# A quantile graph layer: the sorting network's VectorE operations cut to at most 384 elements, the one-element writes between them removed

## The chip, the cores and the metric

The kernel runs on one core of a Trainium2 chip. Its time is the device time of one execution in microseconds (us), the median of several runs; less is better. Besides, one execution is recorded by the hardware profiler; the profile and the trace are that one execution. The engines are called PE (TensorE, matrix products), ACT (ScalarE), DVE (VectorE), POOL (GpSimd) and SP (SyncE, which here only starts DMAs).

## The reference

There are 16 graphs of 1024 nodes with 64 features, a dense adjacency matrix for each (a random edge has a probability of 1/256 in each direction, then the matrix is made symmetric and gets its diagonal), a node mask, and a two-layer perceptron. What is computed, cut to what matters:

```python
h = jnp.maximum(_layernorm(x, axis=-1), 0.0)
# in the graph layer, x is h:
skip = jnp.where(nb > T, (nb + K - 1) // K, 1)          # T, K = 10, 2; nb = number of neighbours
rem = neigh & (sk > 1) & (rank % sk == sk - 1) & mask[:, :, None]
adj_d = jnp.where(rem | jnp.swapaxes(rem, 1, 2), 0.0, adj_)
nd = adj_d > 0
s = jnp.sort(jnp.where(nd[..., None], x[:, None, :, :], jnp.inf), axis=2)
for tau, w in zip((0.25, 0.5, 0.75), (0.25, 0.5, 0.25)):
    pos = tau * jnp.maximum(nd.sum(2) - 1, 0)
    agg = agg + w * (v_lo + frac * (v_hi - v_lo))        # the quantile, interpolated between two sorted values
y = jax.nn.relu((x + agg) @ W1 + b1) @ W2 + b2
out = x_in + y * mask
```

So for each node and each feature, the features of its remaining neighbours are sorted, and three quantiles are mixed.

## The kernel before, in words

**Preparation of a graph** (`load`, `number`, `drop`, `keep`, `order`, `collect`, `normalize`). The adjacency matrix comes in by rows on SP's queue; PE, ACT and DVE drop edges as the reference says and turn what is left into lists of neighbours. The nodes are reordered by degree into 8 blocks of 128, so that a block's nodes need about the same number of list places (`CAPS`: 13 down to 6). DVE finds the lists (L1047, L1087 to L1116); they end as columns of the index tile `idx`. The normalized features go to a table `gtab` in DRAM.

**Gathers.** For each pair of graphs, `fetch` puts one indirect DMA per graph, block and list place on POOL's queue (L1250): 128 rows of 64 floats, named by one column of `idx`, land in one slot of a tile `g`. There are 1008 of them in all. The blocks form four classes, `CLASSES = (((0,), 13), ((1, 2, 3), 11), ((4, 5), 9), ((6, 7), 7))`; a class has one tile `g`, in which a slot holds 128 elements per partition for each of the class's blocks (2 graphs x 64 features): 128, 384, 256 and 256. A few nodes of high degree are handled apart, eight graphs at a time, in a tile `gg` with slots of 128.

**The sort** (`sort`, L1271) runs over a class's tile on DVE. A plan (`PLANS`) is a list of steps; each step names up to three slots to be compared with up to three others, so that one DVE operation handles n slots. A step is a minimum and a maximum (L1288 into a free slot, L1289 in place) or, where only one result is wanted, a single operation (L1285). Then `taken` slots are multiplied by coefficients (L1296), n slots in an operation, and PE adds them into `acc` in PSUM (L1298). Sizes run from 128 to 768 elements per partition, in 32-bit floats.

**The pauses.** After the operations of a step, `let_go` (L1265) looks whether the estimated cost since the last pause has come to 0.8 us; if so it writes a zero into a one-element tile `pause` (L1268), which nobody reads.

**The order of the work.** `weave` mixes the sort of a pair of graphs (`results`, `aggregate`) with the preparation of the next pair, and hands POOL its gathers along the way (`SPREAD` paces them). Afterwards `arrange` (L640) takes all instructions, estimates each one's cost (`Step.cost`), plays the engines' queues through, and fixes the order in which every engine has its instructions. A pause is not a step of its own there: it is kept as the tail of the operation that it follows, adds its cost to it, and is put right behind it in DVE's order.

**The end.** Behind the last pair come the perceptron (`mlp`, `output`), the stores, two indirect stores for each group (L1498), and a flag that says whether any list was too short.

Of the kernel before, what the change touches and what calls it, by code (L numbers as in the profile page):

```python
# [31 lines left out]
F32 = mybir.dt.float32  # L32
# [8 lines left out]
OP = mybir.AluOpType  # L41
AX = mybir.AxisListType

P = 128
N = 1024
C = 64
# [40 lines left out]
BIG = 3.0e38  # L87

SPREAD = 160


FIRST = CAPS[0] - 1
# [508 lines left out]
class Step:  # L601

    def __init__(self, ins, place):
        self.ins, self.place, self.kind = ins, place, type(ins).__name__
        self.engine = NAMES[str(ins.engine).split(".")[-1]]
        self.reads, self.writes = (
            [Use(a.bass_ap) for a in aps if getattr(a, "bass_ap", None) is not None] for aps in (ins.ins, ins.outs)
        )
        self.moves = self.kind == "InstDMACopy"
        self.before, self.behind, self.after, self.tail = set(), set(), [], []  # L610
        self.busy, self.lag = self.cost()

    def cost(self):
# [23 lines left out]
        return 480, 1500 + by / 300  # L637


def arrange(tc, runs, tails=()):  # L640

    steps, found, number = [], {}, {}
    for ins in list(tc.nc.cur_bb.bb.instructions):
        if type(ins).__name__.startswith("BassTile"):
            continue
        if ins.name in tails:
            at = found[tails[ins.name]]
            at.tail.append(ins)
            number[ins.name] = len(number)
            at.busy += Step(ins, 0).busy  # L650
            found[ins.name] = at
            continue
        found[ins.name] = Step(ins, len(steps))
        steps.append(found[ins.name])

    written, read, users, order = {}, {}, {}, {}
    for s in steps:
        for u in s.reads + s.writes:
            name = u.tile.name
            for o, other in written.get(name, ()):  # L660
                if u.meets(other):
                    s.before.add(o.place)
            if u in s.writes:
                for o, other in read.get(name, ()):
                    if u.meets(other):
                        s.before.add(o.place)
        for u in s.writes:
            for table in (written, read):
                table[u.tile.name] = [e for e in table.get(u.tile.name, ()) if not u.covers(e[1])]
            written[u.tile.name].append((s, u))  # L670
        for u in s.reads:
            read.setdefault(u.tile.name, []).append((s, u))
        for u in s.reads + s.writes:
            if getattr(u.tile, "tag", None):
                if u.tile.name not in users:
                    order.setdefault(u.tile.tag, []).append(u.tile)
                users.setdefault(u.tile.name, []).append(s)
    for tiles in order.values():
        for k, t in enumerate(tiles):
            bufs = t.tag_meta.bufs  # L680
            first = users[t.name][0]
            if k:
                first.behind.add(users[tiles[k - 1].name][0].place)
            if k >= bufs:
                first.before.update(o.place for o in users[tiles[k - bufs].name])
            for o in users[t.name][1:]:
                if o is not first:
                    o.behind.add(first.place)
    close = {found[n].place: (found[run[0]].place, found[run[-1]].place) for run in runs for n in run[:-1]}
    for s in steps:  # L690
        for first, last in {close[p] for p in s.before if p in close}:
            if not first <= s.place <= last:
                s.before.add(last)
    for s in steps:
        s.behind -= s.before
        s.before.discard(s.place)
        s.behind.discard(s.place)
        s.left, s.ready = len(s.before) + len(s.behind), 0.0
        for p in (*s.before, *s.behind):
            steps[p].after.append(s)  # L700

    free, wire = dict.fromkeys(ENGINES, 0.0), 0.0
    waiting, able, sequence = ({e: [] for e in ENGINES} for _ in range(3))
    for s in steps:
        if not s.left:
            heappush(waiting[s.engine], (0.0, s.place))
    done = 0
    while done < len(steps):
        when, e = min(
            (free[e] if able[e] else max(free[e], waiting[e][0][0]), e) for e in ENGINES if able[e] or waiting[e]  # L710
        )
        while waiting[e] and waiting[e][0][0] <= when:
            heappush(able[e], heappop(waiting[e])[1])
        s = steps[heappop(able[e])]
        if waiting[e] and waiting[e][0][0] < when + PATIENCE and waiting[e][0][1] < s.place - AHEAD:
            heappush(able[e], s.place)
            free[e] = waiting[e][0][0]
            continue
        done += 1
        sequence[e].append(s)  # L720
        free[e] = when + s.busy
        if e == "SP":
            wire = max(wire, free[e]) + s.lag - 1500
            s.lag = wire + 1500 - free[e]
        for o in s.after:
            if s.place in o.behind:
                least = when
            else:
                least = free[e] + (s.lag + 60 if o.engine != e or s.moves else 115 if e == "DVE" else 0)
            o.ready = max(o.ready, least)  # L730
            o.left -= 1
            if not o.left:
                heappush(waiting[o.engine], (o.ready, o.place))
        for q in ENGINES:
            while waiting[q] and waiting[q][0][0] <= free[q]:
                heappush(able[q], heappop(waiting[q])[1])

    for steps in sequence.values():
        alike = iter(sorted((i for s in steps for i in s.tail), key=lambda i: number[i.name]))
        line = [i for s in steps for i in (s.ins, *(next(alike) for _ in s.tail))]  # L740
        for ins, then in zip(line, line[1:]):
            tc.add_manual_dep(
                then, ins.name, mybir.DependencyInfo(mybir.DependencyClass.NoSync, mybir.DependencyReason.DATA),
                reason="order of the engine",
            )
# [3 lines left out]
def list_layer(  # L749
# [14 lines left out]
    nc = tc.nc  # L764
# [8 lines left out]
    runs = []  # L773
# [444 lines left out]


    pairs = B // 2  # L1220
    tails = {}
    gathered, groups = {}, {}


# [35 lines left out]
                        queue.append(partial(gather, h, slot, k, PASSED[k] + s))  # L1260


    pause = cst.tile([P, 1], F32, name="pause")

    def let_go(held, ins):  # L1265
        if held < 0.8:
            return held
        tails[nc.vector.memset(pause, 0.0).ins.name] = ins.ins.name  # L1268
        return 0.0

    def sort(lines, plan, first, coef, acc):  # L1271

        size = lines.shape[2]
        held = 0.0

        def at(first, step, n):
            stop = first + step * (n - 1) + (1 if step >= 0 else -1)
            return lines[:, first:stop if stop >= 0 else None:step or 1]

        _, _, steps, ends, taken = plan  # L1280
        for n, a, da, b, db, f, df, back, what in steps:
            pa, pb = at(a, da, n), at(b, db, n)
            cost = 0.16 + n * size / 960
            if f < 0:
                ins = nc.vector.tensor_tensor(pa if back else pb, pa, pb, OP.min if what == "min" else OP.max)  # L1285
            else:
                one, other = (OP.min, OP.max) if what == "<" else (OP.max, OP.min)
                nc.vector.tensor_tensor(at(f, df, n), pa, pb, one)  # L1288
                ins = nc.vector.tensor_tensor(pa if back else pb, pa, pb, other)  # L1289
                cost *= 2  # L1290
            yield cost
            held = let_go(held + cost, ins)
        for n in taken:
            now, ends = ends[:n], ends[n:]
            v = at(now[0], now[1] - now[0] if n > 1 else 0, n).rearrange("p s (k c) -> p s k c", c=C)
            ins = nc.vector.tensor_tensor(v, v, coef(first, n)[:, :, :, None].to_broadcast(list(v.shape)), OP.mult)  # L1296
            settle([
                nc.tensor.matmul(  # L1298
                    acc, ident32, lines[:, s], start=False, stop=(s == now[-1] and not ends), skip_group_check=True
                )  # L1300
                for s in now
            ])
            first += n
            cost = 0.16 + n * size / 960
            held = let_go(held + cost, ins)
            yield cost

    def terms(acc, out):
# [283 lines left out]
    fp = psum.tile([1, 1], F32, name="fp", tag="misc")  # L1592
    nc.tensor.matmul(fp, worst, ones_col(cst, nc), start=True, stop=True)
    nc.vector.tensor_scalar(flag, fp, 0.0, None, OP.is_gt)
    arrange(tc, runs, tails)


def ones_col(pool, nc):
# [173 lines left out]
```

## Time and profile before

| what | value |
|---|---|
| time, median of 3 runs | 2607.62 us (2595.87 to 2612.22) |
| the profiled execution's own time | 1581.97 us |
| span of the profiled execution | 1580.2 us |
| granted TensorE clock, mean | 0.841 of full speed |
| DVE busy, instructions | 1191.0 us, 3723 |
| POOL busy, instructions | 1137.8 us, 1051 |
| PE, ACT busy | 1071.0 us, 917.2 us |
| gathers (L1250) | 1008, 1081 ns on the average, from 68.3 to 1516.6 us |
| pauses (L1268) | 578, 59 ns each |

The timed runs and the profiled execution differ by more than a thousand microseconds. The profile describes the second alone. Busy time is the time in which an engine has an instruction under way; an engine with 75% may still be late in one stretch and idle in another. In the groups of instructions, the number behind the bar is the busy time in all and the mean of one in nanoseconds, then the idle time of the engine just before, with what ended it; "issue" means that nothing the profile shows was waited for.

### The profile page before, as it was taken

To read this page: it belongs to the slowest core of one execution; us is meant where nothing else is said; L and a number is where in the kernel's file an instruction comes from. 1 tells how busy PE (TensorE), PEld (TensorE's weight loads), DVE (VectorE), ACT (ScalarE), POOL (GpSimd) and SP (SyncE) were. 2 spreads that over 40 slices of the span, in tenths; PEclk is the share of its full clock that TensorE was granted. 3 is DMA by queue.
4 is the path that set the end of the run, shared out by engine and by line. 5 is a ranking of instruction groups with operands and counts; after the bars stand their busy time and mean duration, and the time that the engine had idled before them with its cause. 6 is when DMAs were issued, how large, how long until landed. Compare 5 with 4: busy or idle time off the path is not lost.

```text
span 1580.2 us, 25600 instructions
## 1 busy us (share of the span) xinstructions
PE 1071.0 (68%) x8385; PEld 664.2 (42%) x8385; DVE 1191.0 (75%) x3723; ACT 917.2 (58%) x2496; POOL 1137.8 (72%) x1051
## 2 busy tenths in 40 slices
PE   6777867889887887888569845588758822602235
PEld 3444544555554555455245534354535412301122
DVE  5615489865997789868884899977988897697660
ACT  6998886987958695978367841766825300200001
POOL 3277776777777777777777777777777777777730
PEclk9989979899998999899679976899888955855568
DMA  6453432442523252325122422222311211211100
GB/s 208 118 159 93 116 110 62 113 116 64 149 69 112 53 149 58 111 59 143 50 71 73 118 78 45 73 84 56 86 28 26 46 31 26 55 24 23 22 11 18
DMA packets 128481, 122.71 MB, mean 78 GB/s; under 512 B 94514, under 2 KB 95026, under 8 KB 128338
## 3 DMA queue, kind: packets, MB, share of 16 engines
q1 hardware_dynamic: 94994, 86.77, 19.4%
q0 software_dynamic: 33344, 34.21, 9.7%
q8 instruction: 68, 1.11, 0.3%
q14 instruction: 75, 0.61, 0.1%
HBM read 110.10 MB, written 9.07 MB: 75 GB/s over the span
## 4 chain that ended last, share of the span: by engine, by line
POOL 32%; ACT 20%; PE 14%; issue 14%; DVE 12%; DMA 6%; DVEq 0%; POOLq 0%; SPq 0%; ACTq 0%
POOL g L1250 31%; PE codeP L1072 5%; DMA g<-gtab,idx 4%; ACT dist L978 4%; ACT sg L891 3%; DVE g L1288 3%; ACT ne L911 3%; DVE g L1289 2%; ACT kept L1001 2%; ACT waste L1170 2%; ACT waste L1165 1%; ACT xt L1178 1%; PE acc L1298 1%; PE rk L968 1%; DMA xt<-in_x_dram 1%
## 5 line engine op out<-in xcount | busy, mean ns | idle before, releaser
L1250 POOL DMA_INDIRECT g<-gtab,idx x1008 | 1089.7, 1081 | 361.3 <-issue 288.0
L1288 DVE TENSOR_TENSOR g<-g 128x512 f32<-128x512 f32 (+3 forms) x408 | 280.7, 701 | 40.9 <-DMA g<-gtab,idx 25.9
L1289 DVE TENSOR_TENSOR g<-g 128x512 f32<-128x512 f32 (+3 forms) x408 | 281.4, 702 | 11.1 <-DMA gg<-g 8.4
L1298 PE MATMUL acc<-g,kf 128*128 128x256 f32 (+2 forms) x448 | 143.4, 461 | 176.5 <-DVE pause L1268 105.2
L1072 PE MATMUL codeP<-pack,perm 128*128 128x332 bf16 x1024 | 185.3, 323 | 21.4 <-DVE perm L1047 18.4
L978 ACT ACTIVATE dist<-rk,bias 128x512 f16<-128x512 f32 x256 | 168.4, 698 | 27.8 <-DVE bias L953 10.7
L1298 PEld LDWEIGHTS acc<-g,kf 128*128 128x128 f32 x448 | 89.5, 231 | 204.1 <-DVE pause L1268 111.4
L968 PE MATMUL rk<-kb,cnt 128*128 128x512 bf16 x256 | 113.2, 442 | 74.5 <-ACT dist L978 68.2
L1001 ACT ACTIVATE kept<-kp 128x512 fp8e4<-128x512 f32 x248 | 149.2, 617 | 14.0 <-PE kp L996 11.9
L898 PE MATMUL tp<-kb,sg 128*128 128x128 bf16 x1024 | 106.8, 243 | 69.3 <-ACT sg L891 52.6
L911 ACT ACTIVATE ne<-tp 128x512 fp8e4<-128x512 f32 x248 | 138.2, 608 | 19.4 <-PE tp L904 10.7
L973 PEld LDWEIGHTS <-ne 128*128 128x128 fp8e4 x1024 | 90.2, 109 | 133.1 <-issue 110.8
L1072 PEld LDWEIGHTS <-perm 128*128 128x128 bf16 x1024 | 93.9, 101 | 85.3 <-DVE perm L1047 43.9
L891 ACT ACTIVATE sg<-at 128x1024 bf16<-128x1024 f32 x121 | 126.6, 1076 | 2.4 <-DMA at<-in_adj_dram 2.3
L898 PEld LDWEIGHTS <-sg 128*128 128x128 bf16 x1024 | 81.2, 110 | 91.1 <-ACT sg L891 61.1
L973 PE MATMUL rk<-kw,ne 128*128 128x128 fp8e5 x1024 | 118.0, 243 | 0.0
L979 DVE TENSOR_SCALAR rem<-dist,half 128x1024 bf16<-128x1024 f16 x128 | 64.7, 506 | 61.7 <-ACT dist L978 60.7
L996 PE MATMUL kp<-kw,rem 128*128 128x128 fp8e5 x1024 | 99.7, 219 | 0.0
L991 PE MATMUL kp<-ne,kw 128*128 128x512 fp8e4 x256 | 98.5, 385 | 0.1
L992 PE MATMUL kp<-rem,kw 128*128 128x512 bf16 x256 | 97.6, 382 | 0.0
L1077 ACT CAST st<-codeP 128x4 bf16<-128x4 f32 x128 | 21.1, 165 | 119.6 <-PE codeP L1072 119.5
L1373 DVE TENSOR_SCALAR at_p<-iota,node 128x512 bf16<-128x512 f16 x256 | 82.8, 370 | 6.8 <-PE low L1397 6.7
(178 smaller groups left out, 2051.1 us busy)
## 6 DMA issues: line engine op xcount, KB each, us to landing
at<-in_adj_dram SPq DMA_DIRECT2D x122, 512.0 KB
g<-gtab,idx POOLq DMA_INDIRECT x1008
xt<-in_x_dram SPq DMA_DIRECT2D x16, 256.0 KB
y<-in_x_dram SPq DMA_DIRECT2D x16, 256.0 KB
gtab<-xt SPq DMA_DIRECT2D x16, 256.0 KB
out_dram<-y SPq DMA_DIRECT2D x16, 256.0 KB
spare<-in_adj_dram SPq DMA_DIRECT2D x6, 512.0 KB
gg<-g SPq DMA_DIRECT2D x32, 48.0 KB
```

The lines of the kernel that those rows point to most:

```text
L891: nc.scalar.activation(sg, at, AF.Sign)
L898: run.append(nc.tensor.matmul(tp[:, s], sg[:, m * P:(m + 1) * P], ident16, start=(s == 0), stop=(s == 3 and t // 4 != n), skip_group_check ...
L911: nc.scalar.activation(to, tp, AF.Relu, saturate=False)
L968: run = [nc.tensor.matmul(rk, cnt[:, ts], blocks[:, 4 * n:4 * n + 4, None].to_broadcast([P, 4, P]), start=True, stop=False, skip_group_che ...
L973: run.append(nc.tensor.matmul(rk[:, s * P:(s + 1) * P], ne[:, 4 * n + s, ts], upper, start=False, stop=(s == 3), skip_group_check=True,))
L978: nc.scalar.activation(dist[:, n * HALF:(n + 1) * HALF], rk, AF.Abs, bias=bias[:, t:t + 1])
L1001: nc.scalar.activation(kept[:, 4 * n:4 * n + 4], kp, AF.Relu, saturate=False)
L1072: run.append(nc.tensor.matmul(flat, perm[:, t, k * P:(k + 1) * P], pack[:, t], start=False, stop=(t == NT - 1), skip_group_check=True,))
L1250: return nc.gpsimd.indirect_dma_start(out=gathered[m, tiles][:, slot, k - lo, h], out_offset=None, in_=tables[2 * m + h][0], in_offset=bas ...
L1288: nc.vector.tensor_tensor(at(f, df, n), pa, pb, one)
L1289: ins = nc.vector.tensor_tensor(pa if back else pb, pa, pb, other)
L1298: nc.tensor.matmul(acc, ident32, lines[:, s], start=False, stop=(s == now[-1] and not ends), skip_group_check=True)
```

## The change

In `sort`, every step is cut into parts of at most `PART // size` slots (at least one), where `size` is the number of elements in a slot. A part does what the step did, for its own slots. With 384 as the limit, a part holds three slots of 128, one of 256 or one of 384. The products are cut in the same way; the matrix products that add them stay together in one run behind all parts. The pauses go, with `let_go`, the tile `pause` and the tails in `arrange`.

```diff
+PART = 384
...
-def arrange(tc, runs, tails=()):
+def arrange(tc, runs):
...
-        if ins.name in tails:
-            at = found[tails[ins.name]]
-            at.tail.append(ins)
-            number[ins.name] = len(number)
-            at.busy += Step(ins, 0).busy
-            found[ins.name] = at
-            continue
...
-        alike = iter(sorted((i for s in steps for i in s.tail), key=lambda i: number[i.name]))
-        line = [i for s in steps for i in (s.ins, *(next(alike) for _ in s.tail))]
+        line = [s.ins for s in steps]
...
-    def let_go(held, ins):
-        if held < 0.8:
-            return held
-        tails[nc.vector.memset(pause, 0.0).ins.name] = ins.ins.name
-        return 0.0
...
+        most = max(1, PART // size)
+
+        def parts(n):
+            return [(k, min(most, n - k)) for k in range(0, n, most)]
+
         for n, a, da, b, db, f, df, back, what in steps:
-            pa, pb = at(a, da, n), at(b, db, n)
-            cost = 0.16 + n * size / 960
-            if f < 0:
-                ins = nc.vector.tensor_tensor(pa if back else pb, pa, pb, OP.min if what == "min" else OP.max)
-            else:
-                one, other = (OP.min, OP.max) if what == "<" else (OP.max, OP.min)
-                nc.vector.tensor_tensor(at(f, df, n), pa, pb, one)
-                ins = nc.vector.tensor_tensor(pa if back else pb, pa, pb, other)
-                cost *= 2
+            for k, many in parts(n):
+                pa, pb = at(a + k * da, da, many), at(b + k * db, db, many)
+                if f < 0:
+                    nc.vector.tensor_tensor(pa if back else pb, pa, pb, OP.min if what == "min" else OP.max)
+                else:
+                    one, other = (OP.min, OP.max) if what == "<" else (OP.max, OP.min)
+                    nc.vector.tensor_tensor(at(f + k * df, df, many), pa, pb, one)
+                    nc.vector.tensor_tensor(pa if back else pb, pa, pb, other)
+            cost = (0.16 + n * size / 960) * (1 if f < 0 else 2)
             yield cost
-            held = let_go(held + cost, ins)
...
-            ins = nc.vector.tensor_tensor(v, v, coef(first, n)[:, :, :, None].to_broadcast(list(v.shape)), OP.mult)
+            for k, many in parts(n):
+                some = now[k:k + many]
+                v = at(some[0], some[1] - some[0] if many > 1 else 0, many).rearrange("p s (k c) -> p s k c", c=C)
+                nc.vector.tensor_tensor(
+                    v, v, coef(first + k, many)[:, :, :, None].to_broadcast(list(v.shape)), OP.mult
+                )
```

More of the change, by code (lines that the diff above doesn't have):

```diff
@@ L609, in __init__ @@
         self.moves = self.kind == "InstDMACopy"
-        self.before, self.behind, self.after, self.tail = set(), set(), [], []
+        self.before, self.behind, self.after = set(), set(), []
         self.busy, self.lag = self.cost()
@@ L637, in cost @@
         return 480, 1500 + by / 300
-def arrange(tc, runs, tails=()):
-    steps, found, number = [], {}, {}
+def arrange(tc, runs):
+    steps, found = [], {}
     for ins in list(tc.nc.cur_bb.bb.instructions):
         if type(ins).__name__.startswith("BassTile"):
-            continue
-        if ins.name in tails:
-            at = found[tails[ins.name]]
-            at.tail.append(ins)
-            number[ins.name] = len(number)
-            at.busy += Step(ins, 0).busy
-            found[ins.name] = at
             continue
@@ L1220, in list_layer @@
     pairs = B // 2
-    tails = {}
     gathered, groups = {}, {}
@@ L1260, in fetch @@
                         queue.append(partial(gather, h, slot, k, PASSED[k] + s))
-    pause = cst.tile([P, 1], F32, name="pause")
-    def let_go(held, ins):
-        if held < 0.8:
-            return held
-        tails[nc.vector.memset(pause, 0.0).ins.name] = ins.ins.name
-        return 0.0
     def sort(lines, plan, first, coef, acc):
         size = lines.shape[2]
-        held = 0.0
         def at(first, step, n):
@@ L1280, in sort @@
         _, _, steps, ends, taken = plan
+        most = max(1, PART // size)
+        def parts(n):
+            return [(k, min(most, n - k)) for k in range(0, n, most)]
         for n, a, da, b, db, f, df, back, what in steps:
-            pa, pb = at(a, da, n), at(b, db, n)
-            cost = 0.16 + n * size / 960
-            if f < 0:
-                ins = nc.vector.tensor_tensor(pa if back else pb, pa, pb, OP.min if what == "min" else OP.max)
-            else:
-                one, other = (OP.min, OP.max) if what == "<" else (OP.max, OP.min)
-                nc.vector.tensor_tensor(at(f, df, n), pa, pb, one)
-                ins = nc.vector.tensor_tensor(pa if back else pb, pa, pb, other)
-                cost *= 2
+            for k, many in parts(n):
[7 more added lines that the diff above has]
+            cost = (0.16 + n * size / 960) * (1 if f < 0 else 2)
             yield cost
-            held = let_go(held + cost, ins)
         for n in taken:
             now, ends = ends[:n], ends[n:]
-            v = at(now[0], now[1] - now[0] if n > 1 else 0, n).rearrange("p s (k c) -> p s k c", c=C)
-            ins = nc.vector.tensor_tensor(v, v, coef(first, n)[:, :, :, None].to_broadcast(list(v.shape)), OP.mult)
+            for k, many in parts(n):
[4 more added lines that the diff above has]
+                )
             settle([
@@ L1304, in sort @@
             cost = 0.16 + n * size / 960
-            held = let_go(held + cost, ins)
             yield cost
@@ L1594, in list_layer @@
     nc.vector.tensor_scalar(flag, fp, 0.0, None, OP.is_gt)
-    arrange(tc, runs, tails)
+    arrange(tc, runs)
 def ones_col(pool, nc):
```

## The prediction

> **What bounds the kernel now.** I read the page first: busy shares, then the chain that ended last.
>
> ```profile
> span 1580.2 us, 25600 instructions
> ...
> PE 1071.0 (68%) x8385; PEld 664.2 (42%) x8385; DVE 1191.0 (75%) x3723; ACT 917.2 (58%) x2496; POOL 1137.8 (72%) x1051
> ...
> POOL 32%; ACT 20%; PE 14%; issue 14%; DVE 12%; DMA 6%; DVEq 0%; POOLq 0%; SPq 0%; ACTq 0%
> ```
>
> POOL leads the chain with 32%, and the 14% of "issue" is mostly POOL's too, as the line's view of the gathers shows (durations in ns: least, median, most; then what the engine sat idle for):
>
> ```profile
> L1250 POOL DMA_INDIRECT g<-gtab,idx x1008: 940/952/2609, 68.3 to 1516.6; - x168
> ...
>   issue: 288.0, 945
>   DVE idx L1116: 55.0, 3
> ```
>
> An undelayed gather costs 0.952 us and the 0.305 us gap behind it (288.0/945), 1.257 in all. From the first gather at 68.3 us to the last at 1516.6 POOL does little but that. So, in the profiled execution, POOL sets the end: 68 us to start, 1449 of gathers, 63 behind the last one. The groups by shape (busy us, mean ns | idle before) give what lengthens them:
>
> ```profile
> L1250 POOL DMA_INDIRECT g<-gtab,idx x1008 | 1089.7, 1081 | 361.3 <-issue 288.0 <-DVE idx L1116 55.0 <-DMA g<-gtab,idx 7.9
> ...
> L1289 DVE TENSOR_TENSOR g<-g 128x768 f32<-128x768 f32 x128 | 121.5, 949 | 0.6
> ...
> L1288 DVE TENSOR_TENSOR g<-g 128x512 f32<-128x512 f32 x136 | 92.6, 685 | 15.1 <-DMA g<-gtab,idx 11.5 <-issue 3.2
> ...
> L1296 DVE TENSOR_TENSOR g<-g,coef 128x768 f32<-128x768 f32 x64 | 59.2, 950 | 0.1
> ...
> L1289 DVE TENSOR_TENSOR g<-g 128x384 f32<-128x384 f32 x88 | 47.9, 550 | 8.6 <-DMA gg<-g 8.4
> ...
> L1268 DVE MEMSET pause<- 128x1 f32 x578 | 34.1, 59 | 0.0
> ```
>
> The gathers' mean is 1081 ns against a median of 952, so waits inside them come to 1008 x 0.129 = 130 us. For whom, the timeline says (start, us):
>
> ```profile
> 240.98 0.95 DVE L1289 TENSOR_TENSOR g<-g 128x768 f32<-128x768 f32 x1
> 241.86 0.68 DVE L1288 TENSOR_TENSOR g<-g 128x512 f32<-128x512 f32 x1
> 241.88 0.06 DVE L1268 MEMSET pause<- 128x1 f32 x1
> 242.47 0.95 DVE L1288 TENSOR_TENSOR g<-g 128x768 f32<-128x768 f32 x1
> 243.34 0.19 DVE L1174 RECIPROCAL var<-var 128x8 f32<-128x8 f32 x1
> 243.45 0.64 DVE L1289 TENSOR_TENSOR g<-g 128x512 f32<-128x512 f32 x1
> ...
> 242.18 1.19 POOL L1250 DMA_INDIRECT g<-gtab,idx  x1 [0.30 <-issue]
> 243.67 1.24 POOL L1250 DMA_INDIRECT g<-gtab,idx  x1 [0.30 <-issue]
> ```
>
> The gather of 242.18 ends at 243.37, 0.83 us after the DVE operation then under way ended (242.54), although the next DVE operation had already begun at 242.47. The one of 243.67 ends at 244.91, 0.82 after the L1289 operation of 243.45 (0.64 us long) ended. A gather waits for the end of the DVE operation in flight and gets in there, in the profiled execution, whether or not a pause follows.
>
> **The timed runs are another matter.** The profiled execution took 1581.97 us, 1.8 more than its span; the median of the timed runs is 2607.62, 1026 more. Nothing in the trace is 1026 us long. A sum comes near: if POOL and DVE hardly overlapped there, the time would be 68 + POOL's 1038 indirect DMAs (1008 g, 26 gg, 4 gx) x 1.257 = 1305 + DVE's 1138 of busy time in the stretch of the gathers + 63 = 2574, 34 short of the median. That POOL and DVE exclude each other in the timed runs is an inference from this sum; no view shows it.
>
> [...] Here 384 more elements take 949 - 550 = 399 ns, 1.04 each, which leaves 149 ns fixed, of which about 80 lie under the operation before (241.86 + 0.68 = 242.54 against the start at 242.47: 0.07; others 0.08): 0.07 us net[...]. [...] I count 1.257 for a gather, not 0.952 (242.18 to 243.67 is 1.49, which leaves 0.23 of wait, as its 1.19 - 0.952 does).
>
> **The change part by part.**
>
> Splitting. The limit counts slots of the class: one slot of 384 elements (class 1, 2, 3), one of 256 (classes 4, 5 and 6, 7), three of 128 (class 0; the group's gg too). So the operations of 768 become two of 384 or, in 32 of L1296's 64, three of 256; those of 512 become two of 256; 384 and below stay. More operations: 256 + 272 + 32 + 2 x 32 = 624. By busy time 256 x (2 x 0.550 - 0.949) = 39, 272 x (2 x 0.418 - 0.685) = 41, 32 x 0.150 = 5, 32 x (3 x 0.415 - 0.950) = 9: 94 us. By time on the engine, with the overlap of neighbours, 624 x 0.07 = 44. I take 44; the ends are 44 and 94.
>
> Pauses. 578 writes of 59 ns, 34 us busy. With one between them, neighbours still overlap: the operation of 240.98 ends at 241.93, the next starts at 241.86, the same 0.07. So a pause occupies about 0.01 us: 6 us are won; ends 0 and 34. Nobody reads the tile. DVE, net: 44 - 6 = +38 us, between +10 and +94.
>
> Cover. In the profiled execution DVE has 389 us idle, which hides 38; with that cover gone (behind the last gather, and in the stretches where DVE is over 90% busy) they count in full.
>
> POOL's wait. A gather that comes at random waits half an operation, in proportion to its length, so the wait goes with the sum of squares. Over the rows[...]: 768: 320 x 0.90 = 288; 512: 272 x 0.47 = 128; 384 about 99; 256 about 38; the TENSOR_SCALARs of L979, L1047 and L1373 about 98; the rest about 30: 680. Splitting takes a third of 288 (two parts leave 0.67, three 0.58: 97 off) and a quarter of 128 (33 off): 130/680 = 19%, so 19% of 130 = 25 us in the profiled execution. There the change should win: 1580 - 25 + a few us at the tail = about 1558.
>
> The order. The planner orders every engine by costs; it now sees 624 more DVE steps and no longer adds the pauses' busy time. No DMA or wait is added, and nothing is moved past a queue by hand. I cost a different order at zero, +-10.
>
> **The sum for the timed runs.** Under exclusion DVE's 38 us lie beside nothing and count in full. [...] 578 x 0.059 = 34 us of opening at most, of which I take 20 as lost to POOL[...]. 2607.6 + 38 + 20 = 2666, say 2665.
>
> **Rivals.**
>
> *The pauses are the doors.* In the timed runs, POOL gets in where DVE asks for nothing, and loses at an ordinary boundary between two operations. Then without pauses a whole run of back-to-back operations bars POOL, and of 578 doors each lost one costs up to one gather, 1.257 us. With a tenth to a third lost: 578 x 0.1 to 0.33 x 1.257 = 73 to 240 us, with DVE's 38: 2720 to 2885; middle 2790. For it: 1026 us that are missing from the trace. Against: in the trace POOL gets in at ordinary boundaries.
>
> *The wait is behind single operations (faster).* Place: L1250's start, behind L1288, L1289, L1296. If the timed runs wait as the traced one does, only more, the waits are 130 + 1026 = 1156 us and 19% of it is 220; DVE's 38 come off: 2607 - 182 = 2425. If half of the 1026 is such wait: 19% of 643 = 122, less 38: 2523. Middle 2500. It decides from the point where the waits behind single operations exceed 38/0.19 = 200 us. For it: the grants at the very end of an operation in the timeline. Against: 1156 us over 1008 gathers are 1.15 each, longer than the longest of these operations.
>
> *Nothing moves.* The 1026 us have to do with neither engine's pairing (each gather simply takes longer), POOL stays the bound, DVE's 38 are hidden and the 25 of wait cancel against the tail: 2590 to 2625. That the change does little of what it says is part of this: 384 and 256 were below the limit before, and only 592 of the exchanges and 64 products are cut.
>
> **How the numbers follow.** Exclusion 0.41 (2635 to 2700), doors 0.23 (2700 to 2890), single operations 0.24 (2400 to 2580), nothing 0.12. The likeliest gives 2665. For 8 in 10 the range goes into both outer cases: low 2480 leaves out some 0.10, high 2810 some 0.09. One per cent (26 us) is about what a measurement can tell from no change here: the three runs span 16. Slower: 0.41 + 0.23 less a little at the edge, 0.62; within 1%: 0.14; faster 0.24.
>
> **What would show it.** In the changed kernel's profile: 3723 + 624 - 578 = 3769 DVE instructions; DVE busy near 1191 + 94 - 34 = 1251; no L1268 row, no 768 or 512 rows of g; the gathers' mean near 1.056 us with the same median; a span near 1558. If the profile gains these 25 us while the timed median rises, exclusion or doors is right; if the median falls by much more than the profile, single operations. I would be wrong if the timed runs' 1026 us depend on the length of one DVE operation, and wholly so if short operations free POOL altogether.

## The result, and the profile after

The changed kernel takes 2677.61 us (median of 4 runs, 2674.79 to 2683.86); the kernel before took 2609.92 us beside it (4 runs, 2595.87 to 2621.63). The ratio is 1.0249, with a 95% interval of 1.0211 to 1.0286: slower by 2.5%, 68 us.

A ratio with its interval is made, unless it is said otherwise, from the runs within 1.5% of a kernel's fastest, a median from all of its runs. The numbers come from two kinds of chip. The kernel before takes 2574 to 2619 us (medians) on most of the chips used here and 1576 to 1588 us on another, and the runs of before on any one chip lie within 1.5% of one another; the profile shown ahead of the prediction came, by its 1581.97 us, from the second kind, the timed runs and most of what follows from the first. I call them the 2600 chips and the 1580 chips. What makes them different no run says.

The page of the changed kernel, from a 2600 chip, has the span, the busy times and the shares of the chain that ended last:

```profile
span 2673.2 us, 25690 instructions
...
PE 1162.3 (43%) x8371; PEld 707.8 (26%) x8385; DVE 1222.8 (46%) x3769; ACT 925.2 (35%) x2496; POOL 1044.7 (39%) x1051
...
another core or an unknown queue 34%; DVE 18%; ACT 18%; PE 17%; issue 11%; DMA 2%; POOL 0%; DVEq 0%; SPq 0%; POOLq 0%; ACTq 0%
```

Its profiled execution took 2675.28 us, so this time span and timed runs describe the same thing. No engine is busy for half of it, POOL has left the chain, and for a third of the span the chain waits for something that the trace doesn't name. The kernel runs on one core, so that isn't another core. It has 3769 DVE instructions, as forecast. The groups by shape (busy us, mean ns | idle before):

```profile
L1242 POOL DMA_INDIRECT g<-gtab,idx x1008 | 999.6, 992 | 1328.8 <-PE acc L1289 636.3 <-issue 322.1 <-DVE idx L1109 245.2
...
L1277 DVE TENSOR_TENSOR g<-g 128x384 f32<-128x384 f32 x344 | 183.3, 551 | 16.4 <-DMA gg<-g 4.8 <-remote 3.6 <-PE acc L1329 2.6
...
L1276 DVE TENSOR_TENSOR g<-g 128x256 f32<-128x256 f32 x328 | 129.5, 419 | 7.6 <-issue 4.9 <-DVE g L1276 1.0 <-DVE g L1277 1.0
...
L1285 DVE TENSOR_TENSOR g<-g,coef 128x256 f32<-128x256 f32 x104 | 39.2, 417 | 1.0 <-DVE g L1277 1.0
```

The 768 and 512 shapes are gone and the shorter ones have the durations the prediction read in the old trace. The gathers sit idle 1329 us, of which 636 wait for PE.

To know what of that is the change, the kernel before must be seen on the same kind of chip. A run of it there (label e10_before_third below) has this page:

```profile
span 2614.7 us, 25586 instructions
...
PE 1165.2 (45%) x8371; PEld 707.0 (27%) x8385; DVE 1184.4 (45%) x3723; ACT 928.3 (36%) x2496; POOL 1043.4 (40%) x1051
...
another core or an unknown queue 32%; ACT 18%; DVE 17%; PE 15%; issue 15%; DMA 2%; POOL 0%; DVEq 0%; SPq 0%; POOLq 0%; ACTq 0%
```

The pattern is the same before the change, and so is the work. Engine busy times are those of the 1580 chip within 10%; they lie beside each other far less. The view of one stretch shows how (start:end, length, then busy us with counts of PE, PEld, DVE, ACT and POOL, granted clock, DMA share, GB/s). The kernel before on a 1580 chip:

```profile
690.00:770.00 80.00, 61.02 (x525) 37.60 (x523) 64.24 (x185) 61.98 (x148) 62.93 (x57) 0.92 0.41 110
```

The same kernel on a 2600 chip:

```profile
690.00:770.00 80.00, 14.68 (x60) 8.75 (x58) 9.36 (x25) 9.35 (x30) 59.16 (x62) 0.57 0.17 32
```

The changed kernel on a 2600 chip:

```profile
690.00:770.00 80.00, 17.31 (x65) 9.65 (x64) 12.04 (x39) 12.21 (x37) 60.49 (x65) 0.59 0.16 31
```

On the 1580 chip every engine works beside the gathers. On the 2600 chips POOL gathers at its usual pace (62 to 65 in 80 us) while PE, DVE and ACT nearly stand still (9 to 17 us busy of the 80). The timeline of the changed kernel shows how such a stretch ends (start, length; in brackets the idle time before and its releaser):

```profile
551.39 0.44 PE L1065 MATMUL codeP<-pack,perm 128*128 128x332 bf16 x2
...
591.54 0.94 POOL L1242 DMA_INDIRECT g<-gtab,idx  x1 [0.30 <-issue]
...
599.48 0.16 ACT L1070 CAST st<-codeP 128x4 bf16<-128x4 f32 x1 [44.11 <-remote]
...
599.96 0.65 DVE L1080 MAX8 keys<-codeP 128x8 f32<-128x128 f32 x2 [52.55 <-ACT own L1075]
...
600.99 0.10 PEld L1061 LDWEIGHTS <-kb 128*128 128x128 bf16 x1 [46.24 <-issue]
```

PE's products into codeP are through at 551.8, yet the ACT cast that reads them starts at 599.48, 7.0 us after the last gather of the batch ended (591.54 + 0.94); DVE and PE follow within about 1.5 us. From 551.58 to 592.48, 33 gathers ran back to back. The three products that send PE's signal (its semaphore update) in this stretch end at 551.70, 551.84 and 552.06; the trace records PE's next three signals at 599.46, 599.49 and 599.55, while PE itself went on with other products until 555.15.

So I split each span by the start and end times in the traces into gather time (each of POOL's indirect DMAs with the 0.31 us behind it) and the rest, and took the time that DVE is busy in each (time in which two instructions overlap counted once, as in the page's busy time), in us:

| trace | chip | span | gather time | DVE in it | DVE outside it | neither |
|---|---|---|---|---|---|---|
| before (e5) | 1580 | 1575.8 | 1442 | 1133 | 59 | 75 |
| before (e10) | 2600 | 2614.7 | 1349 | 331 | 853 | 412 |
| after (e9) | 2600 | 2676.6 | 1351 | 315 | 907 | 419 |

Between the last two rows, from the same chip, the span grows by 62: gather time +2, DVE outside it +53, neither +7 (by unrounded figures). DVE's own total grows by 37 (1184 to 1221), and 16 us less of it lies beside gathers.

### The profile page after: what moved, and what is told of

The parts are those of the page before. It is cut to its first block, busy times and chain, and to the rows that moved or that the text cites. A ratio compares the mean times of both kernels' runs of the same rounds, so it can differ in the third digit from the quotient of the medians.

```text
span 2673.2 us, 25690 instructions
## 1 busy us (share of the span) xinstructions
PE 1162.3 (43%) x8371; PEld 707.8 (26%) x8385; DVE 1222.8 (46%) x3769; ACT 925.2 (35%) x2496; POOL 1044.7 (39%) x1051
## 4 chain that ended last, share of the span: by engine, by line
another core or an unknown queue 34%; DVE 18%; ACT 18%; PE 17%; issue 11%; DMA 2%; POOL 0%; DVEq 0%; SPq 0%; POOLq 0%; ACTq 0%
DVE g L1276 5%; DVE g L1277 5%; PE codeP L1065 4%; ACT dist L971 3%; ACT sg L884 2%; ACT kept L994 2%; ACT ne L904 2%; PE acc L1289 2%; DVE gg L1276 1%; DVE gg L1277 1%; PE rk L966 1%; PE tp L891 1%; ACT waste L1163 1%; PE rk L961 1%
## 5 line engine op out<-in xcount | busy, mean ns | idle before, releaser
L1242 POOL DMA_INDIRECT g<-gtab,idx x1008 | 999.6, 992 | 1328.8 <-PE acc L1289 636.3
L1277 DVE TENSOR_TENSOR g<-g 128x384 f32<-128x384 f32 (+1 forms) x672 | 311.7, 486 | 51.3 <-remote 31.3
L1276 DVE TENSOR_TENSOR g<-g 128x384 f32<-128x384 f32 (+1 forms) x672 | 309.9, 487 | 13.4 <-issue 8.3
L1289 PE MATMUL acc<-g,kf 128*128 128x256 f32 (+2 forms) x448 | 152.2, 475 | 194.8 <-DVE g L1285 190.7
L891 PE MATMUL tp<-kb,sg 128*128 128x128 bf16 x1024 | 115.9, 256 | 249.7 <-issue 101.2
L1065 PE MATMUL codeP<-pack,perm 128*128 128x332 bf16 x1024 | 194.6, 335 | 4.3 <-DVE perm L1040 3.8
L1422 DVE TENSOR_TENSOR yp<-yp,mask 128x256 f32<-128x256 f32 x32 | 13.7, 429 | 316.3 <-remote 171.4
L966 PE MATMUL rk<-kw,ne 128*128 128x128 fp8e5 x1024 | 127.0, 253 | 0.0
L997 PE MATMUL code<-kw,kept 128*128 128x17 fp8e5 x1024 | 65.5, 173 | 138.3 <-issue 80.9
L1080 DVE MAX8 keys<-codeP 128x8 f32<-128x128 f32 x128 | 38.0, 297 | 185.7 <-ACT own L1075 124.1
L984 PE MATMUL kp<-ne,kw 128*128 128x512 fp8e4 x256 | 105.9, 414 | 28.1 <-ACT dist L971 28.0
```

The lines of the kernel that those rows point to most:

```text
L891: run.append(nc.tensor.matmul(tp[:, s], sg[:, m * P:(m + 1) * P], ident16, start=(s == 0), stop=(s == 3 and t // 4 != n), skip_group_check ...
L966: run.append(nc.tensor.matmul(rk[:, s * P:(s + 1) * P], ne[:, 4 * n + s, ts], upper, start=False, stop=(s == 3), skip_group_check=True,))
L1065: run.append(nc.tensor.matmul(flat, perm[:, t, k * P:(k + 1) * P], pack[:, t], start=False, stop=(t == NT - 1), skip_group_check=True,))
L1242: return nc.gpsimd.indirect_dma_start(out=gathered[m, tiles][:, slot, k - lo, h], out_offset=None, in_=tables[2 * m + h][0], in_offset=bas ...
L1276: nc.vector.tensor_tensor(at(f + k * df, df, many), pa, pb, one)
L1289: nc.tensor.matmul(acc, ident32, lines[:, s], start=False, stop=(s == now[-1] and not ends), skip_group_check=True)
```

## The experiments

Runs of one chip are compared only with the kernel before on that chip; its medians there were 2612.6 us (chip A), 1580.62 (B), 2618.74 (C) and 2574.03 (D).

**Each half of the change alone (chip A).** First the cut, with the one-element writes kept where they were:

```
+            for k, many in parts(n):
+                pa, pb = at(a + k * da, da, many), at(b + k * db, db, many)
...
             held = let_go(held + cost, ins)
```

> The cut at 384 elements alone; the pauses stay behind each step, 578 or so. Exclusion (POOL's gathers and the other engines take turns, so DVE time counts in full): the 624 extra operations cost 44 us, so about 2654 against 2610. Doors (pauses let POOL in): no pause is lost, so within 15 us of before plus the 44, but then the change's other run, pauses gone alone, must carry a cost of its own. Single operations: faster than before by over 50 us.

Measured: 2680.23 us, 1.0268 times before (1.021 to 1.0326). That is all of the loss. With the writes or without them, the cut kernel takes about the same; the 20 us set for the openings that the pauses leave aren't there in the time. Inside the gathers they can be seen:

```profile
L1251 POOL DMA_INDIRECT g<-gtab,idx x1008 | 973.5, 966 | 1358.9 <-PE acc L1310 680.8 <-issue 323.7 <-DVE idx L1117 252.6
```

The mean of a gather is 966 ns here and 992 in the changed kernel, 26 us over all 1008, and no gather takes over 2.1 us. But DVE is busy beside gathers for only 262 us here, against 324 in the first trace of the changed kernel, so what POOL gains isn't gained by the whole.

Then the writes left out, with the operations whole:

```
-        if held < 0.8:
+        if held < 1e9:
```

> The pauses alone are left out; operations keep up to 768 elements. Exclusion with pauses that do next to nothing: 2604, that is 0 to 10 us faster than before. My sum's 20 us of openings lost: 2624. Doors: 2680 or more.

Measured: 2645.87 us, 1.0142 (1.0086 to 1.0199). Without the pauses this kernel has 578 DVE instructions fewer and no other ones, and is slower by 1.4%. But one thing more has changed: the planner no longer adds a pause's cost to the step ahead of it, and orders the engines differently. This is taken apart below.

**Is it the gathers? (chip A)** The 1008 gathers replaced by plain loads of 128 neighbouring table rows, issued by SP; the lookup through the index lists is left out, so other rows arrive, and no load waits for an index list.

```
-                return nc.gpsimd.indirect_dma_start(
...
+                table, first = tables[2 * m + h][0], tables[2 * m + h][1] // C + FRONT + at
+                return nc.sync.dma_start(out=gathered[m, tiles][:, slot, k - lo, h], in_=table[first:first + P])
```

> Leaves out the lookup: each of the 1008 gathers becomes a plain load of 128 neighbouring rows of the same table into the same slot, issued from SP's queue; the number of transfers, of bytes and of landings stays. Theory turn-taking is caused by POOL making the gathers: the freezes of the other engines go, and the time comes to 1350 to 1650. Rival, the landings of 1008 transfers and their semaphore counts hold up the other engines: still over 2200. [...]

Measured: 1520.83 us, 0.583 (0.5795 to 0.5865). The stretch that stood still before:

```profile
690.00:770.00 80.00, 70.94 (x559) 41.68 (x558) 65.42 (x220) 63.14 (x189) 0.00 (x0) 0.97 0.40 102
```

PE, DVE and ACT work for 63 to 71 of the 80 us, with 102 GB/s moved in all, the loads into the same tiles among them. The standstill goes with the indirect transfers that POOL issues and not with the bytes. It also settles whether a lower clock makes these chips slow: the mean granted TensorE clock is 0.69 to 0.70 in the runs of before on this chip and 0.859 in this one, so the low clock goes with the standstill and isn't the chip's own.

The same for the second graph of each pair only, 504 gathers staying on POOL (`if h:` ahead of the load; the lookup is left out for that half):

> As the run with all loads on SP, but only for the second graph of a pair; 504 gathers stay on POOL (their lookup is right, the others' is left out). Turn-taking: each gather that is left costs the others about 1.25 us of standing still, so halfway between the kernel before and the run with no gathers, near 2000. Landings: no change against before.

Measured: 1954.99 us, 0.7485 (0.7435 to 0.7534). The first 504 gathers removed give 658 us, 1.30 each; the other 504 give 434, 0.86 each. One gather with the gap behind it takes 1.25. So the first half taken away saves its whole length, as if it lay beside nothing; of the rest a third is hidden.

**The kernel before once more, for its trace.** The chip fell to the 1580 kind.

> The kernel before, unchanged, for a second trace. Turn-taking in the timed runs: near 2610, with DVE nearly idle while POOL's gathers run, other than in the first profile, where DVE was busy for 1138 of the gathers' 1449 us. If the first profile showed the kernel as it is timed, DVE is about as busy there as it was.

Measured: 1577.55 us. Every one of the 7 runs of before on this chip took 1576 to 1588 us. The 1026 us between the first profile and the timed runs are therefore a difference of chips, not of a profiled and an unprofiled execution.

**The writes left out, with every engine's order kept.** The planner still charges a pause to the step ahead of where it stood; only the write isn't issued:

```
         if ins.name in tails:
+            found[ins.name].busy += (1 + 66) / 0.96
...
-        tails[nc.vector.memset(pause, 0.0).ins.name] = ins.ins.name
+        tails[ins.ins.name] = True
```

> No pauses, whole operations, and the planner still charges a pause's cost at each place, so that every engine keeps the order of the kernel before. If the 33 us of the run without pauses come from the new order: within 15 us of before, 2597 to 2627. If they come from the missing openings on DVE: again 2640 or more.

Measured on chip B: four runs from 1618.46 to 1659.9 us, 1643.63 in the middle, 1.0391 (1.0299 to 1.0483, over all four). Here the pauses are worth 38 to 79 us; the runs scatter too much to say it closer. The profiled run is the shortest, 38 us above before's median. The timeline of POOL and DVE shows what they prevent:

```profile
1277.36 0.94 POOL L1250 DMA_INDIRECT g<-gtab,idx  x1 [0.30 <-issue]
...
1278.44 1.41 DVE L1289 TENSOR_TENSOR g<-g 128x384 f32<-128x384 f32 x2
1278.61 22.26 POOL L1250 DMA_INDIRECT g<-gtab,idx  x1 [0.30 <-issue]
1279.77 1.42 DVE L1288 TENSOR_TENSOR g<-g 128x384 f32<-128x384 f32 x2
...
1297.77 0.95 DVE L1289 TENSOR_TENSOR g<-g 128x768 f32<-128x768 f32 x1
1298.63 1.42 DVE L1288 TENSOR_TENSOR g<-g 128x384 f32<-128x384 f32 x2
1301.18 0.94 POOL L1250 DMA_INDIRECT g<-gtab,idx  x1 [0.31 <-issue]
```

A gather that usually takes 0.95 us takes 22.26, while 34 DVE operations follow each other, each starting before the last has ended; it ends 0.82 us after the last of them (1298.63 + 1.42 = 1300.05 against 1300.87). In the three traces of the kernel before, and in that of the cut kernel with pauses, no gather took over 2.62 us. By the means of the groups, this trace has (1117 - 1080) x 1008 = 37 us more waiting inside gathers than e5's; the one above is 21 of it. The span of this trace is 41 us longer than e5's (1616.8 against 1575.8), so the waits are most of that.

The same kernel went to chip D, beside the next one:

> Whole operations, no pauses, every engine's order as in the kernel before. On a chip where the kernel before takes 2610: within 15 us of it if the 33 us of the run without pauses came from the new order, 2640 or more if they came from the missing pauses themselves. On one where it takes 1580: about 1644 again.

Measured there: 20 runs from 2526.66 to 2585.58 us. Their median is 2559.53, 0.9944 of before's; the 12 shortest alone give 0.9887 (0.9853 to 0.9921). The same code that loses 2 to 5% on a 1580 chip wins about 1% on a 2600 one, where its longest gather took 4.7 us. The gathers' mean is longer than before's on a 2600 chip (e10), and yet the time is shorter:

```profile
L1250 POOL DMA_INDIRECT g<-gtab,idx x1008 | 998.2, 990 | 1266.7 <-PE acc L1298 415.3 <-issue 294.3 <-DVE idx L1116 232.0
...
L1250 POOL DMA_INDIRECT g<-gtab,idx x1008 | 1017.4, 1009 | 1195.5 <-PE acc L1298 358.1 <-issue 294.0 <-DVE idx L1116 224.7
```

The first line is e10's, the second this run's. The waits inside gathers grow by 19 us, but DVE is busy beside gathers for 417 us instead of 331. The two traces come from two chips, which may account for part of it.

> The changed kernel once more. On a chip where the kernel before takes 2610: 2677 a third time, nothing new. On one where it takes 1580: 1558 by my sum for the profiled execution (shorter operations, shorter waits); 1600 to 1650 by the doors theory, with single gathers that wait ten microseconds or more, as in the run without pauses there.

Measured on chip D: 2661.13 us, 1.0322 (1.0271 to 1.0372) for the changed kernel, 0.7% more than in the two other comparisons. So the whole operations without pauses, in the old order, beat both kernels there (2559.5 against 2574.0 and 2661.1). It isn't a better kernel everywhere, as chip B shows.

**What on POOL makes the others stand still?** Two kernels ask this. One is e3 with POOL kept busy, writing zeros four times into each slot before its load:

```
+                for _ in range(4):
+                    nc.gpsimd.memset(to, 0.0)
+                return nc.sync.dma_start(out=to, in_=table[first:first + P])
```

> As the run with all loads on SP (the lookup left out), and POOL writes zeros four times into each slot ahead of its load, so that it is busy with some 4000 small operations that start no transfer. If any busy POOL makes the others stand still: over 2000. If it takes POOL's own transfers: within 150 us of the run with loads on SP, 1520 to 1670.

The other has e3's plain loads issued by POOL (`nc.gpsimd.dma_start`); both leave the lookup out.

> Leaves out the lookup too, but the 1008 plain loads are issued by POOL. If transfers started by POOL make the others stand still, with or without an index: over 2200. If it takes the reading of the index column: near the run with loads on SP, under 1700.

Measured: 1469.76 us, 0.9292 (0.9243 to 0.9341), and 1520.21 us, 0.9611 (0.956 to 0.9662). Both ran on chip B, where nothing stands still to begin with, so neither can answer: whether it takes POOL's starting of a transfer, the index read or a busy POOL stays open. They say one thing: on that chip all gathers together, with what waits for them, are worth 60 to 111 us, against 1092 on chip A. That plain loads take 1520 us on both chips, issued by SP on A and by POOL on B, is a hint that the chips differ in little else.

**Before and after, traced on one 2600 chip (C).**

> The changed kernel, unchanged, beside the kernel before. Two chips have been seen so far: on one the kernel before takes 2610 us, on the other 1580. On the first: 2677 again. On the second, where POOL and DVE overlap, my sum for the profiled execution gives 1558, since waits behind operations of up to 768 get shorter; the doors theory[...] gives 1600 to 1650, as the run without pauses did there (1644).

> The kernel before, unchanged, for a trace on this chip. On the first chip: near 2610, with DVE hardly busy while POOL's gathers run, under 400 us of overlap. On the second: 1580, as in the two traces that there are.

Measured: 2679.03 us for the changed kernel, 1.025 (1.0185 to 1.0315), and 2616.38 us in the one run of before. The table above is from these two traces. POOL's idle time before the gathers grows with the span, from 1266.7 to 1332.6 us. The largest part of it is waiting for PE. The kernel before, in the view of waits (who waits for whom: us, count, longest):

```profile
POOL g L1250 <- PE acc L1298: 415.3, 10, 77.4
...
POOL g L1250 <- PE rk L973: 106.1, 1, 106.1
POOL g L1250 <- PE tp L898: 100.4, 1, 100.4
```

The changed kernel:

```profile
POOL g L1242 <- PE acc L1289: 653.8, 11, 106.1
```

Two of the long waits are put down to other PE lines before the change, so the two are alike: 622 us in 12 waits before, 654 in 11 after. The other 34 us of idle time are spread over DVE and "issue". So POOL, too, is late by some 60 us, at a handful of waits for other engines; which instruction ahead of them made them longer was not traced.

And a gather behind one of these waits shows that long waits inside gathers come back without pauses here too, though it is one in 1008:

```profile
526.32 14.01 POOL L1242 DMA_INDIRECT g<-gtab,idx  x1 [18.31 <-PE acc L1289]
540.63 0.94 POOL L1242 DMA_INDIRECT g<-gtab,idx  x1 [0.31 <-issue]
```

For this whole wait DVE operations overlap, as in e6. Without the 0.82 us it ends at 539.51 (526.32 + 14.01 - 0.82), and there, for the first time in it, the next operation starts later than the one before ended, by 0.04 us.

## Why the prediction was right, and where it wasn't

The forecast was 2665; 2677.6 is well inside its range and on its side. Its larger term, DVE's work counted in full, was right; that the sum came so near is partly luck, since a wrong term of 20 us stood where other losses of about that size were. Point by point:

- **What bounds the kernel.** The reading "POOL sets the end" holds for the chip that made the first profile, and only there: POOL falls from 32% of the chain to 0% on the other. The gap of 1026 us, which the prediction had put down to the timed runs, is the chip's.
- **POOL and DVE exclude each other.** Right in its effect: on a 2600 chip 331 of DVE's 1184 us lie beside gathers (28%), against 1133 of 1192 (95%) on the other. Its sum came near 2607 by offset errors: it counted 1138 us of DVE where 853 lie outside gather time, and 131 us of start and tail where 412 belong to neither. And the waits behind DVE's operations, 130 us in the first profile, don't account for it: inside the gathers they are (990 - 947) x 1008 = 43 us there, and PE and ACT stand still too (14.68 and 9.35 us busy of the 80 above). What the traces do show is what the gathers in these waits end with: of those that took over 1.15 us, 249 of 273 in the first profile and 55 of 69 in the changed kernel's trace end 0.82 us, to within 0.015, after the end of an operation on DVE. No run ties the standstill to that.
- **Splitting and pauses, DVE +38.** Right: 624 more operations and 578 fewer writes raise DVE's busy time from 1184.4 us (e10) to 1221.3 (e9), by 37. The durations of the single instructions add up to 1399.5 and 1458.0, 59 more. The prediction's 94 - 34 = 60 is such a sum of durations, and it was wrong to add it to a page's busy time, which counts overlapped time once; so the 1251 forecast for a profile was too high. (Its 592 cut exchanges include the 64 products; the exchanges alone are 528.)
- **The cover.** Right that on these chips the 38 lie beside nothing. All 37 and 16 more come to lie outside the gathers: 53 of the span's 62.
- **20 us of openings lost with the pauses.** Wrong, and this is the step that failed: it counted waits inside gathers as time. The waits are there, in the size set for them: 26 us between e1's trace and the changed kernel's (their orders differ), 19 between e10's and e12's (one order, two chips). But in the traces without pauses more of DVE's work lies beside gathers (324 us against 262, 417 against 331), and the time doesn't follow. With the operations cut, keeping the pauses wins nothing (1.0268 against 1.0249, intervals overlapping); with the operations whole and the order kept, leaving them out wins 14 us on chip D by the medians. What stood in place of the 20 was 16 us less of DVE beside gathers, 7 in which neither worked and 2 of gather time.
- **The order, at zero +-10.** Wrong, at least for whole operations. e2 and e12 are the same instructions in two orders: 1.0142 against 0.9887 to 0.9944, a difference of 2.0 to 2.6%, some 50 to 67 us. The ratios are from two chips, each against before there, and the change itself gives ratios 0.7% apart on chips C and D, so this is a rough size. In the traces ACT's 2496 instructions stand in e12 all in the order of the kernel before; to restore that order, 375 would have to be moved in e2, 356 in the changed kernel and 390 in e1. So the cut reordered the kernel about as much as leaving out the pauses did, and e1 doesn't separate the two either. A cut kernel in the old order wasn't run. Where the time lies argues for the work rather than the order: e2's time outside the gathers is 30 us longer than e10's with DVE's share of it about the same (849 against 853), while 53 of e9's 60 us more are DVE's. That is an argument, not a proof, so how the 68 us divide between cut and order stays open.
- **The profiled execution at 1558.** Not tested: the changed kernel never came to a 1580 chip. On a 2600 chip the mean of a gather didn't fall (990 to 992 ns); few gathers meet DVE there, and a 14 us wait eats what shorter operations save.

The rivals. **Doors** has the 1580 chip for it, where leaving the pauses out costs 38 us or more, but in the traced run over half of it is one gather's wait of 22 us, not a gather lost at every third to tenth door; on the 2600 chips it is worth nothing that can be seen in the time. **Single operations** fell: what waits there is 43 us, and 19% of it, 8 us, can't pay for 38. **Nothing moves** fell with an interval that begins at 1.0211; its premise, that the 1026 us had to do with neither engine's pairing, was half right, since PE and ACT stand still as DVE does.

## What to carry to other kernels

When a profiled execution and the timed runs differ by 65%, don't build a bridge between them: look for a profile that has the time you are to explain, since the two can come from chips on which the same kernel is limited by different things (here POOL had 32% of one chain and 0% of the other). The 37 us that the change added to DVE came back in full where the other engines didn't run beside it (53 us more outside the gathers), so ask of every engine what actually overlaps there, not what could. And before crediting an edit, hold the order of the other instructions fixed: reordering alone was worth about as much here as the change.

## What the runs showed of the hardware

- On the 2600 chips POOL's back-to-back indirect DMAs (1.25 us apart) go along with PE, ACT and DVE nearly standing still: 17.31, 12.21 and 12.04 us busy of 80 in the changed kernel, 14.68, 9.35 and 9.36 in e10. In the stretch shown around 551 to 600 us they start again 7 us after the last of the batch, and a cast waited 44 us for products that the trace shows finished; behind the other batches of 20 or more in that trace it took 0.3 to 12.7 us. Replacing the 1008 gathers by loads from SP took 2612.6 us to 1520.8. Late signals fit this: in the changed kernel's trace 120 of PE's 1242 recorded signals come over 2 us after the newest end, as the trace has it, of a product that sends one, in e10's 119, in e3's on the same kind of chip 11, in the first profile of before 2. Why they are late isn't shown, and the two runs meant for it were made on a 1580 chip.
- A gather that starts while DVE runs operations without a gap can wait for a whole row of them: 22.26 us in e6, behind 34 of them, and 14.03, 14.01 and 13.79 us in three traces of the changed kernel. In the four traces with the one-element writes (e1 and three of before) the longest gather took 2.61 us. An ordinary boundary, at which the next operation starts before the last has ended, often lets a gather in, and sometimes doesn't: of the 55 gathers of the changed kernel's trace named above, 41 end 0.82 us after such a boundary, while in the wait of 14.03 us 29 operations of DVE ended without letting the gather in. The three waits of 14 us, the longest of e2 (6.5) and the longest of e12 (4.7) all end at the first place where two operations don't overlap, 0.03 to 0.04 us wide; but a gather of 3.48 us in e9 went past such a place. What decides isn't known.
- Cutting an operation in two costs about 0.07 us, as read from one trace before: 624 x 0.07 less 578 x 0.01 is 38, and 37 were measured. The 578 writes, 34 us by their durations, take 3 us of DVE's busy time (1184.4 in e10 against 1181.0 in e12).
